# The square root's seed moved to ScalarE, and the channels' direct way turned into a diagonal product

## The chip, the cores and the metric

The kernel runs on one core of a Trainium2 chip. The metric is the device time of one launch in microseconds (us). A core has five engines that run their own queues of instructions in order: PE (matrix products; PEld is its loading of weights), DVE (vector), ACT (scalar, with activation functions), POOL (general purpose) and SP, which here only issues transfers (DMA).

## The reference, cut to what matters

The first layer is a state-space block, done twice (`NLAYERS = 2`) on 4 batches of 4096 positions with 96 channels. Inside, there are 192 channels and 16 states for each:

```
mu = seq.mean(-1, keepdims=True)
var = ((seq - mu) ** 2).mean(-1, keepdims=True)
h = (seq - mu) * jax.lax.rsqrt(var + EPS) * ln_g + ln_b
xz = h @ in_w
xs, z = jnp.split(xz, 2, axis=-1)
...
xc = jax.nn.silu(xc)                      # after a causal convolution of 4 taps
delta = jax.nn.softplus(dt @ dt_w + dt_b)
dA = jnp.exp(delta[..., None] * A)
dBx = delta[..., None] * Bm[:, :, None, :] * xc[..., None]
hstates = jax.lax.associative_scan(comb, (dA, dBx), axis=1)[1]
y = jnp.einsum('blds,bls->bld', hstates, Cm) + Dp * xc
y = y * jax.nn.silu(z)
return y @ out_w
```

The change is in two places of this: `rsqrt(var + EPS)`, and the term `Dp * xc`, the channels' direct way past the states. A quadratic layer and two pairs of Fourier and feed-forward layers follow. The change does not touch them.

## The kernel before, in words

The function `_mamba` holds the state-space stage. The work is cut into 32 units `(ch, l, pr)`: a chunk of 512 positions (`TC`), a layer, and a pair of batches. The channels of a pair fill three groups `k` of 128 partitions: `k = 0` and `1` hold the first 128 channels of either batch, `k = 2` the last 64 of both.

A unit is scanned in 24 steps: three groups `k`, four rounds `r`, two halves `h`. A step does this:

- SP loads a copy of `delta` spread over the states into a tile `a` (`copies`, line 434), and ACT turns it into the decay `exp(delta * A)` (`decays`, line 452).
- PE spreads `delta * xc` over the states into a PSUM tile `pq` of two banks, of which there are three (`broadcasts`, line 447). DVE multiplies it by `B` (`product`, line 457). In the steps with `k < 2`, `h = 0` and odd `r` ("apart"), a loaded copy `db` is multiplied on POOL instead, and ACT writes the decay into the `pq` tile.
- DVE runs two scans over 512 positions into `hs` (`scans`, line 470). POOL multiplies the states by `C` into `hc` (line 476). Both `hs` and `hc` have two tiles of two steps each.
- ACT keeps the last state for the next chunk (`states`, `hst`, line 480), and PE sums the states into the channels with a matrix `red`, four products into four quarters of one PSUM tile `py` (`reduce`, line 488). There is one `py` tile; it is summed over eight steps.
- After the eighth, `gate` reads it. DVE makes `y = Dp * xcv + py` (line 496), and POOL multiplies by `silu(z)` (line 497). The gates of the three groups come at the steps 10, 18 and 2 of the next unit.

Beside the steps run other chains, cut into pieces by `yield`; `Side.slot` lets one piece through in each step. `norm` makes the normalised input of a coming unit: PE subtracts the mean and sums the squares (`mm_v`, line 212), ACT adds epsilon (`ve`, line 221), DVE makes the seed of the inverse square root by shifting the bits of the float (lines 223 to 225, `it`, `r`, `vh`), and POOL refines it three times (lines 227 to 230); PE spreads the result (`mm_r`, line 240), and DVE multiplies (`hn`, line 249). `front` multiplies by the input weights (`mm_i`, lines 264 and 267), ACT empties each bank into `xcv` and `zs` (lines 275 and 277), and then come SiLU (lines 279 and 280), the products `mm_dbl` (lines 287 and 290), `delta` (line 315 and softplus, line 601), and `du`, `ux`, `uy` and `ul` (lines 339 to 355), which feed the spreading of `delta * xc`. `tail` multiplies by the output weights (`mm_o`, lines 369 to 371; the results are `s` or `ft`). `xcv` has two tiles. All products of `norm`, `front` and `tail` share one PSUM bank, `mm`.

The order on every engine is the order in which the program is written (`manual_schedule`). SP's queue issues nearly all transfers, so a transfer that waits for its data holds back those behind it; the copies of `ul` into `ux` and `uy` (line 345) are such.

Of the kernel before, what the change touches and what calls it, by code (L numbers as in the profile page):

```python
# [9 lines left out]
F32 = mybir.dt.float32  # L10
F32R = mybir.dt.float32r
I32 = mybir.dt.int32
# [3 lines left out]
AF = mybir.ActivationFunctionType  # L16
ALU = mybir.AluOpType
# [6 lines left out]
NL = 2  # L24
# [3 lines left out]
TC = 512  # L28
# [14 lines left out]
def _load(nc, pool, src, shape, name, dtype=F32):  # L43
    t = pool.tile(shape, dtype, name=name, tag=name)
    nc.sync.dma_start(t, src)
    return t


def _mamba(ctx, tc, io, w, fd, fstats, xsums):
# [9 lines left out]
    nc = tc.nc  # L59
    wp = ctx.enter_context(tc.tile_pool(name="mw", bufs=1))  # L60
# [5 lines left out]
    ps_y = ctx.enter_context(tc.tile_pool(name="mpsy", bufs=1, space=PSUM))  # L66
    vec, ident = w["vec"], w["ident"]
# [23 lines left out]
    red = _load(nc, wp, io["k_red"].rearrange("c (j m) -> c j m", j=4), [128, 4, 32], "red")  # L91
    ctr = _load(nc, wp, io["k_center"], [C, C], "ctr")
    low = _load(nc, wp, io["k_low"], [128, 2], "low")
    mean1 = wp.tile([C, 1], F32, name="mean1", tag="mean1")
    nc.gpsimd.memset(mean1, 1.0 / C)

# [56 lines left out]
    def col(l, n, k):  # L153

        at = l * 6 + n * 2 + (k == 2)
        return pv[:, at : at + 1]


    units = []
    for ch in range(NCH + 1):  # L160
# [6 lines left out]
    seq, made, ys = {}, {}, {}  # L167
    pqs, das, dbs, hss, hcs, pys = {}, {}, {}, {}, {}, {}

    def tag(unit):  # L170
        return "_".join(map(str, unit))

    def mm(nm, unit, shape=None):
        return ps_mm.tile(shape or [128, TC], F32, name=f"mm_{nm}{tag(unit)}", tag="mm")

    def tl(nm, unit, shape, dtype=F32, bufs=1, to=None):
        return work.tile(shape, dtype, name=f"{nm}_{tag(unit)}", tag=to or nm, bufs=bufs)
# [9 lines left out]
    def norm(unit):  # L187

        ch, l, pr = unit
        bs = (2 * pr, 2 * pr + 1)  # L190
        xc, sqs, ps = {}, {}, {}

        def centred(n):
            xc[n] = tl(f"xc{n}", unit, [C, TC])
            nc.scalar.copy(xc[n], ps[n])
            sqs[n] = tl(f"sq{n}", unit, [C, TC])
            nc.scalar.activation(sqs[n], xc[n], AF.Square)

        for n, b in enumerate(bs):
            ps[n] = mm(f"xc{n}", unit, [C, TC])  # L200
            nc.tensor.matmul(ps[n], ctr, seq[b, ch, l], start=True, stop=True)
            if l == 0:
                nc.scalar.activation(
                    tl("xs", unit, [C, TC], to=f"sq{n}"), seq[b, ch, 0], AF.Identity, accum_out=xsums[:, b, ch : ch + 1]
                )
            yield
            centred(n)
            yield "free" if n == 0 else "gap"
        p_v = mm("v", unit, [128, 8])
        for n in range(2):  # L210
            for j in range(4):
                nc.tensor.matmul(
                    p_v[:, n * 4 + j : n * 4 + j + 1], sqs[n][:, j * 128 : (j + 1) * 128], mean1, start=True, stop=True
                )
        yield
        ve = tl("ve", unit, [128, 8])
        it = tl("it", unit, [128, 8], I32)
        r = tl("r", unit, [128, 8])
        vh = tl("vh", unit, [128, 8])
        a = tl("ra", unit, [128, 8])  # L220
        nc.scalar.activation(ve, p_v, AF.Identity, bias=w["eps"])
        yield "gap"
        nc.vector.tensor_single_scalar(it, ve.bitcast(I32), 1, op=ALU.logical_shift_right)
        nc.vector.tensor_scalar(r.bitcast(I32), it, -1.0, float(0x5F3759DF), ALU.mult, ALU.add)
        nc.vector.tensor_scalar(vh, ve, -0.5, None, ALU.mult)
        for _ in range(3):
            nc.gpsimd.tensor_tensor(a, r, r, ALU.mult)
            nc.gpsimd.tensor_tensor(a, a, vh, ALU.mult)
            nc.gpsimd.tensor_scalar(a, a, 1.5, None, ALU.add)
            nc.gpsimd.tensor_tensor(r, r, a, ALU.mult)  # L230
        if ch:
            for b in bs:
                hn = hn_buf[b, l]
                nc.scalar.copy(hn[:, 0:3], hn[:, TC:])
        yield "gap"
        yield "gap"
        for n, b in enumerate(bs):
            p = mm(f"r{n}", unit, [C, TC])
            for j in range(4):
                nc.tensor.matmul(  # L240
                    p[:, j * 128 : (j + 1) * 128],
                    r[:, n * 4 + j : n * 4 + j + 1].to_broadcast([128, C]),
                    ident,
                    start=True,
                    stop=True,
                )
            yield
            yield
            nc.vector.tensor_tensor(hn_buf[b, l][:C, 3:], p, xc[n], ALU.mult)
            yield "free"  # L250
# [159 lines left out]
    def name(s):  # L410
        unit, k, r, h = steps[s]
        return f"{tag(unit)}_{k}_{r}_{h}"
# [69 lines left out]
    def reduce(g):  # L482
        unit, k, r, h = steps[2 * g]
        if r == 0:
            pys[unit, k] = ps_y.tile([128, TC], F32, name=f"py_{name(2 * g)}", tag="py")
        hc = hcs.pop(g)
        for i in range(4):
            nc.tensor.matmul(  # L488
                pys[unit, k][32 * (i // 2 + i % 2 * 2) :][:32], red[:, r, :], hc[:, i, :], start=(r == 0), stop=(r == 3)
            )  # L490

    def gate(g):
        unit, k, r, h = steps[2 * g]
        xcv, zs = made[unit][0:2]
        y = work.tile([128, TC], F32, name=f"y{k}_{name(2 * g)}", tag=f"y{k}")
        nc.vector.scalar_tensor_tensor(y, xcv[:, k, :], col(unit[1], 2, k), pys.pop((unit, k)), ALU.mult, ALU.add)
        (nc.gpsimd if 2 * g + 2 < n_steps else nc.vector).tensor_tensor(y, y, zs[:, k, :], ALU.mult)
        ys[unit, k] = y

# [34 lines left out]
    with tc.manual_schedule():  # L534
        for n in (0, 1):
            load(units[n])
        side.front = [weights(0), norm(units[0]), front(units[0])]
        side.drain()
        for s in range(5):
# [7 lines left out]
        for s in range(n_steps + NS):  # L547
# [5 lines left out]
            if at == 0:  # L553
                if n + 1 < len(units) and n + 1 not in late:
                    side.front += ([norm(units[n + 1])] if n == 0 else []) + [front(units[n + 1])]
                    side.norm += [weights(1)] * (n == 0)
            if at == 22 and n + 1 == len(units):
                side.tail.append(way_out(units[n]))
            if at == 3 and 0 < n < len(units):
                if n + 1 in late:  # L560
                    side.front = [tail(units[n - 1]), norm(units[n + 1]), front(units[n + 1])]
                else:
                    side.tail.append(tail(units[n - 1]))
# [5 lines left out]
            if s + 2 < n_steps:  # L569
                unit, k, r, h = steps[s + 2]  # L570
# [9 lines left out]
            if s % 2 == 1 and 2 < s <= n_steps + 1:  # L580
                reduce(s // 2 - 1)
# [5 lines left out]
            if live and s + 5 < n_steps:  # L587
                unit, k, r, h = steps[s + 5]
# [5 lines left out]
            if s % 8 == 2 and 2 < s <= n_steps + 2:  # L594
                gate(s // 2 - 2)
# [800 lines left out]
@with_exitstack  # L1396
def kernel(ctx: ExitStack, tc: tile.TileContext, io, out):
    nc = tc.nc
    cp = ctx.enter_context(tc.tile_pool(name="common", bufs=1))
    dp = ctx.enter_context(tc.tile_pool(name="scratch", bufs=1, space=DRAM))  # L1400
    w = _shared(nc, cp, io)
    p2 = [[dp.tile([2 * C, TC], F32, name=f"p2_{b}_{n}", tag=f"p2_{b}_{n}") for n in range(NCH)] for b in range(B)]
    fd = [dp.tile([C, L], F32, name=f"fd_{b}", tag=f"fd_{b}") for b in range(B)]
    with tc.tile_pool(name="stats", bufs=1) as fp:
        fstats = fp.tile([C, B, NCH, 6], F32, name="fstats", tag="fstats")
        xsums = fp.tile([C, B, NCH], F32, name="xsums", tag="xsums")
        with ExitStack() as c:
            _mamba(c, tc, io, w, fd, fstats, xsums)
        with ExitStack() as c:
            _back(c, tc, io, w, fd, fstats, xsums, p2, out)  # L1410
# [143 lines left out]
```

## Time and profile before

| what | value |
|---|---|
| time, median of 3 runs | 5290.37 us (5288.55 to 5313.22) |
| the profiled execution's own time | 5277.23 us |
| its span in the profile | 5275.4 us |
| mean TensorE clock granted over the span | 0.802 |
| PE busy | 4055.2 us, 77% |
| DVE busy | 4432.0 us, 84% |
| ACT busy | 2695.1 us, 51% |
| POOL busy | 2988.1 us, 57% |

The page gives the busy time of each engine, the span in slices, the transfers, the chain of work that ended last, and the costliest groups of instructions. A group's line has the line of the code, the engine, the operation, output and inputs, their shapes, and the count; then the busy time in us, the mean of one in ns, and the idle time of the engine just before, with what ended it. The state-space stage takes some 3125 us of the span; the table's shares are over all stages.

### The profile page before, as it was taken

The page shows a single profiled execution, that of the slowest core. Times are in us where ns is not written, and L with a number is a line of the kernel's source. Part 1 is how long each engine was busy: PE and PEld are TensorE (multiplying, and loading weights), DVE is VectorE, ACT ScalarE, POOL GpSimd, SP SyncE. Part 2 cuts the span into 40 slices and gives each one's busy share as a digit, 9 for nine tenths or more (in the row PEclk, how much of TensorE's full clock was granted, in tenths as well). Part 3 has the DMA queues.
Part 4 walks back from the last instruction along what each step waited for, and adds up shares of the span by engine and source line. Part 5 has one row for each costly group of instructions (what it writes and reads, how often), then busy time and mean ns, then how long its engine had stood idle before and what let it go on. Part 6 is the DMA issues. An engine that isn't in the chain of part 4 may idle for free.

```text
span 5275.4 us, 52716 instructions
## 1 busy us (share of the span) xinstructions
PE 4055.2 (77%) x15440; PEld 1763.8 (33%) x15440; DVE 4432.0 (84%) x5735; ACT 2695.1 (51%) x5085; POOL 2988.1 (57%) x2104
## 2 busy tenths in 40 slices
PE   4676767777777777777777636899898889989776
PEld 2122222222222222222222102345454555545565
DVE  2879999999999999999999777878787978787655
ACT  3465656656565565656656420023453545444566
POOL 2778888888888888888888761002130312112122
PEclk7677767677786777767777658999999999999976
DMA  4778878788888878788788674553324233322110
GB/s 99 171 171 197 198 187 203 194 196 201 197 192 195 200 190 194 189 195 202 184 201 202 148 192 139 171 170 100 99 85 145 90 102 94 98 90 76 57 33 21
DMA packets 314045, 800.18 MB, mean 152 GB/s; under 512 B 52247, under 2 KB 58106, under 8 KB 312702
## 3 DMA queue, kind: packets, MB, share of 16 engines
q1 hardware_dynamic: 310174, 790.53, 59.2%
q10 hardware_dynamic: 3584, 6.29, 0.4%
q8 instruction: 123, 2.02, 0.2%
q14 instruction: 164, 1.34, 0.1%
HBM read 703.83 MB, written 67.63 MB: 146 GB/s over the span
## 4 chain that ended last, share of the span: by engine, by line
PE 26%; DVE 26%; issue 17%; ACT 11%; POOL 8%; DMA 5%; SPq 1%; DVEq 0%; POOLq 0%; ACTq 0%
DVE hs L470 12%; PE py L895 10%; DVE pq L457 6%; ACT a L452 3%; DMA a<-ddl 3%; POOL hc L476 3%; PE mm_i L264 2%; DVE z L880 2%; DVE a L1110 2%; PE px L1177 2%; PE ph L1092 2%; PE pa L1078 2%; PE py L488 1%; POOL t L1248 1%; POOL o L1246 1%
## 5 line engine op out<-in xcount | busy, mean ns | idle before, releaser
L476 POOL TENSOR_TENSOR hc<-hs,bc 128x1024 f32<-128x1024 f32 x767 | 1804.8, 2360 | 365.8 <-DVE hs L470 350.0
L470 DVE TENSOR_TENSOR_SCAN hs<-a,hst,pq 128x512 f32<-128x512 f32 x1280 | 1571.9, 1261 | 28.9 <-ACT hst L480 12.8
L895 PE MATMUL py<-z,wk 128*96 128x512 f32 x2304 | 1113.5, 613 | 25.8 <-issue 14.3
L452 ACT ACTIVATE a<-a,aneg 128x512 f32<-128x512 f32 x1280 | 849.4, 712 | 309.5 <-DMA a<-ddl 307.4
L880 DVE TENSOR_TENSOR z<-cp,cp 128x512 f32<-128x512 f32 x1152 | 792.5, 714 | 183.9 <-PE py L895 169.3
L457 DVE TENSOR_TENSOR pq<-pq,bc 128x1024 f32<-128x1024 f32 x640 | 772.9, 1208 | 156.9 <-PE pq L447 156.9
L488 PE MATMUL py<-hc,red 128*32 128x512 f32 x3072 | 609.0, 865 | 14.3 <-POOL hc L476 14.3
L895 PEld LDWEIGHTS py<-z,wk 128*96 128x96 f32 x2304 | 366.5, 169 | 447.7 <-issue 315.6
L447 PE MATMUL pq<-uy,sel 64*128 64x512 f32 x768 | 253.4, 654 | 257.1 <-DVE hs L470 204.7
L1145 POOL MEMSET zz<- 96x2 f32 x16 | 1.6, 98 | 740.8 <-ACT zz L1154 739.4
L264 PE MATMUL mm_i<-hn,wk 97*128 97x512 f32 x512 | 348.7, 817 | 92.5 <-ACT xcv L275 59.7
L1246 POOL TENSOR_TENSOR o<-o,fb 128x384 f16<-128x384 f16 x64 | 70.1, 1096 | 549.4 <-ACT o L1251 549.4
L470 DVE TENSOR_TENSOR_SCAN hs<-pq,hst,db 128x512 f32<-128x512 f32 x256 | 324.8, 1269 | 58.1 <-issue 36.1
L452 ACT ACTIVATE pq<-a,aneg 128x512 f32<-128x512 f32 x256 | 177.1, 692 | 366.6 <-DVE hs L470 336.4
L457 POOL TENSOR_TENSOR db<-db,bc 128x1024 f32<-128x1024 f32 x128 | 301.8, 2358 | 21.8 <-DMA db<-ddu 20.3
L447 PE MATMUL pq<-ux,sel 64*128 64x512 f32 x512 | 166.4, 637 | 186.1 <-DVE hs L470 171.8
L447 PEld LDWEIGHTS pq<-uy,sel 64*128 64x128 f32 x768 | 93.8, 238 | 550.8 <-DVE hs L470 372.1
L264 PEld LDWEIGHTS mm_i<-hn,wk 97*128 97x128 f32 x512 | 117.2, 254 | 297.3 <-issue 204.2
L1177 PE MATMUL px<-bd,a 128*96 128x128 f32 x1024 | 148.6, 294 | 67.5 <-DVE a L1110 57.1
L1146 POOL TENSOR_TENSOR zz<-zz 96x256 f32<-96x256 f32 x128 | 122.3, 955 | 135.5 <-ACT zz L1153 83.4
L447 PEld LDWEIGHTS pq<-ux,sel 64*128 64x128 f32 x512 | 61.4, 232 | 384.7 <-DVE hs L470 275.4
L275 ACT ACTIVATE xcv<-mm_i,pvec 128x512 f32<-128x512 f32 x96 | 65.8, 685 | 213.8 <-PE mm_i L264 108.8
(286 smaller groups left out, 6645.8 us busy)
## 6 DMA issues: line engine op xcount, KB each, us to landing
a<-ddl SPq DMA_DIRECT2D x768, 512.0 KB, 7.3
cp<-p SPq DMA_DIRECT2D x480, 192.0 KB, 2.7
db<-ddu SPq DMA_DIRECT2D x128, 512.0 KB, 7.6
bc<-ddb SPq DMA_DIRECT2D x64, 512.0 KB, 8.4
cp<-p SPq DMA_DIRECT2D x480, 64.0 KB, 2.6
ddl<-dl SPq DMA_DIRECT2D x128, 192.0 KB, 3.5
tw_k_fwd<-in_k_fwd SPq DMA_DIRECT2D x64, 256.0 KB, 3.6
tw_k_inv<-in_k_inv SPq DMA_DIRECT2D x64, 256.0 KB, 3.0
```

Of the source, the lines that this page charges most:

```text
L264: nc.tensor.matmul(p, wt[:, 0:128], hn_buf[bs[k], l][:, cols], **f)
L447: nc.tensor.matmul(pqs[s][:, i, :], sel[rows, r, :], made[unit][6][k][h][rows], start=True, stop=True)
L452: nc.scalar.activation(to[:, i, :], das[s][:, i, :], AF.Exp, scale=acol(s, i))
L457: engine.tensor_tensor(t, t, bc(unit, 2, k, h), ALU.mult)
L470: nc.vector.tensor_tensor_scan(hss[g][:, at, :], d0[:, i, :], d1[:, i, :], hst[pr, l, g % 12][:, at : at + 1], ALU.mult, ALU.add)
L476: (nc.gpsimd if s + 1 < n_steps else nc.vector).tensor_tensor(hcs[g][:, sl, :], hss[g][:, sl, :], bc(unit, 3, k, h), ALU.mult)
L488: nc.tensor.matmul(pys[unit, k][32 * (i // 2 + i % 2 * 2) :][:32], red[:, r, :], hc[:, i, :], start=(r == 0), stop=(r == 3))
L880: nc.vector.tensor_tensor(zs[n], cps[q, r0], cps[q, r1], ALU.mult)
L895: nc.tensor.matmul(pys[q], wk[k // KG][:, k % KG, :], zs.pop(n), start=(k == 0), stop=(k == NE - 1))
L1146: nc.gpsimd.tensor_tensor(z0[:, :, 0, :], z0[:, :, 0, :], z1[:, :, 0, :], ALU.add)
L1177: nc.tensor.matmul(p[:, j, :], a2[i % 2][:, kk, :], tabs["bd"][:, int(kk > 0), :], start=True, stop=True)
L1246: nc.gpsimd.tensor_tensor(o2.rearrange("p j c -> p (j c)"), os.pop(g), d["fb2"], ALU.add)
```

## The change

Three things are different.

The seed of the inverse square root is made by ACT. It was an integer shift, a subtraction from a constant and a scaling on DVE; it is now one activation that reads the float's bits as an integer, multiplies by -0.5 and adds the constant, which is a column `magic`. `vh` (minus half of the variance) is made by ACT too, in the same piece as `ve`.

The direct term becomes a product on PE. A table `skip` is built once on POOL: for each layer, and for `k < 2` and `k = 2`, the 128 values of `Dp` stand on the diagonals of four 32 by 32 blocks. `reduce` opens the sum of each `py` tile with four products of such a block with 32 rows of `xcv`; the products with `red` then add to it.

`gate` has only to copy `py` out, and ACT does that; POOL's multiplication follows as before.

```diff
+    magic = wp.tile([128, 1], F32, name="magic", tag="magic")
+    nc.gpsimd.memset(magic, float(0x5F3759DF))
...
+    skip = wp.tile([128, 2 * NL, 32], F32, name="skip", tag="skip")
+    for l in range(NL):
+        for k in (0, 2):
+            for q in range(4):
+                rows = slice(32 * q, 32 * q + 32)
+                nc.gpsimd.tensor_scalar(skip[rows, 2 * l + k // 2, :], ident[rows, rows], col(l, 2, k)[rows], None, ALU.mult)
...
         ve = tl("ve", unit, [128, 8])
-        it = tl("it", unit, [128, 8], I32)
...
         nc.scalar.activation(ve, p_v, AF.Identity, bias=w["eps"])
+        nc.scalar.activation(vh, ve, AF.Copy, scale=-0.5)
         yield "gap"
-        nc.vector.tensor_single_scalar(it, ve.bitcast(I32), 1, op=ALU.logical_shift_right)
-        nc.vector.tensor_scalar(r.bitcast(I32), it, -1.0, float(0x5F3759DF), ALU.mult, ALU.add)
-        nc.vector.tensor_scalar(vh, ve, -0.5, None, ALU.mult)
+        nc.scalar.activation(r.bitcast(I32), ve.bitcast(I32), AF.Identity, bias=magic, scale=-0.5)
...
         if r == 0:
-            pys[unit, k] = ps_y.tile([128, TC], F32, name=f"py_{name(2 * g)}", tag="py")
+            p = pys[unit, k] = ps_y.tile([128, TC], F32, name=f"py_{name(2 * g)}", tag="py")
+            for q in range(4):
+                rows = slice(32 * q, 32 * q + 32)
+                nc.tensor.matmul(p[rows], skip[rows, 2 * unit[1] + (k == 2), :], made[unit][0][rows, k, :], start=True, stop=False)
...
-                pys[unit, k][32 * (i // 2 + i % 2 * 2) :][:32], red[:, r, :], hc[:, i, :], start=(r == 0), stop=(r == 3)
+                pys[unit, k][32 * (i // 2 + i % 2 * 2) :][:32], red[:, r, :], hc[:, i, :], start=False, stop=(r == 3)
...
-        nc.vector.scalar_tensor_tensor(y, xcv[:, k, :], col(unit[1], 2, k), pys.pop((unit, k)), ALU.mult, ALU.add)
+        nc.scalar.copy(y, pys.pop((unit, k)))
```

Apart from these, the instructions of every engine stand in the order in which they stood before, and SP's queue is the same instruction for instruction. The bursts of four products come at the steps 3, 11 and 19 of a unit, right ahead of the first products with `red`; ACT's copies come at the steps 10, 18 and 2, right behind a copy of the last state.

## The prediction

> **What bounds the kernel now.** I read in this order: stretches of 500 us, groups by line, the list of waits, then the order of time in one unit. A unit is the work on one chunk of two batches in one layer; it takes 24 steps, and a step is two decayed copies, one product and two scans.
>
> First the stretches. Columns: bounds, length, busy us (instructions) of PE, PEld, DVE, ACT, POOL, then clock, DMA share, GB/s.
> ```profile
> 500.00:1000.00 500.00, 377.16 (x1287) 123.58 (x1291) 474.73 (x419) 297.35 (x506) 435.21 (x267) 0.73 0.83 198
> 1500.00:2000.00 500.00, 371.32 (x1266) 124.21 (x1259) 472.78 (x419) 300.11 (x513) 435.57 (x280) 0.71 0.83 197
> ```
> The reader sees DVE busy 95% and POOL 87%, while ACT has 40% to spare. The whole change lies in this stage, which ends near 3125 us; the rest of the 5275 us is untouched. On these two lines alone, taking work off DVE should pay in full.
>
> Then the groups that the change removes (busy us, mean ns, idle before).
> ```profile
> L496 DVE SCALAR_TENSOR_TENSOR y<-xcv,pvec,py 128x512 f32<-128x512 f32 x96 | 69.5, 723 | 4.2 <-PE mm_o L369 2.5 <-PE py L488 1.6
> L224 DVE TENSOR_SCALAR r<-it 128x8 int32<-128x8 int32 x32 | 62.3, 1946 | 1.1
> L225 DVE TENSOR_SCALAR vh<-ve 128x8 f32<-128x8 f32 x32 | 33.8, 1056 | 0.0
> L223 DVE TENSOR_SCALAR it<-ve 128x8 int32<-128x8 int32 x32 | 24.8, 775 | 32.2 <-ACT ve L221 32.2
> ```
> Three instructions on 8 columns cost 120.9 us, though the first unit's, with POOL idle, took 0.17 us each. In later units they stand behind POOL's long products.
>
> Last, one unit in order of time, with its step 18 ending at 2433.4. Start, us, operation, and in brackets the idle time before it. POOL, without the small refinement instructions between 2439.7 and 2443.0:
> ```profile
> 2434.91 2.35 POOL L476 TENSOR_TENSOR hc<-hs,bc 128x1024 f32<-128x1024 f32 x1
> 2437.22 1.26 POOL L497 TENSOR_TENSOR y<-y,zs 128x512 f32<-128x512 f32 x1
> 2438.43 1.27 POOL L339 TENSOR_TENSOR du<-dl,xcv 128x512 f32<-128x512 f32 x1
> ...
> 2443.02 2.35 POOL L476 TENSOR_TENSOR hc<-hs,bc 128x1024 f32<-128x1024 f32 x1
> ...
> 2450.09 4.86 POOL L476 TENSOR_TENSOR hc<-hs,bc 128x1024 f32<-128x1024 f32 x2
> 2454.90 1.27 POOL L355 TENSOR_TENSOR ul<-du,ux 128x512 fp32r<-128x512 f32 x1
> ```
> POOL has no gap from 2430.1 to 2456.2, just where DVE makes the seed. The third `ul` ends at 2456.2; behind it stand four `ux`/`uy` copies on SP's queue, then the load of `a` for step 5 of the next unit (2459.7). ACT must decay that before it empties the front's first bank (line 275). PE follows:
> ```profile
> 2467.85 3.78 PE L264 MATMUL mm_i<-hn,wk 97*128 97x512 f32 x4 [1.49 <-ACT xcv L275]
> 2471.56 0.80 PE L447 MATMUL pq<-uy,sel 64*128 64x512 f32 x2
> 2472.29 1.93 PE L488 MATMUL py<-hc,red 128*32 128x512 f32 x8
> ...
> 2502.85 0.79 PE L447 MATMUL pq<-uy,sel 64*128 64x512 f32 x2
> 2503.57 1.93 PE L488 MATMUL py<-hc,red 128*32 128x512 f32 x8
> 2505.44 1.08 PE L287 MATMUL mm_dbl<-xcv,xp 128*64 128x512 f32 x4
> 2506.45 1.08 PE L290 MATMUL mm_dbl<-xcv,xp 64*64 64x512 f32 x4
> ```
> DVE waits for `pq` at 2472.4, 2479.6 and 2503.7 (0.72, 1.01, 3.62 us) and at 2510.35 (1.90 us) for a scan buffer that ACT's `hst` copy releases; on ACT that copy stands behind the emptying of `mm_dbl`. So from the front's first bank (about step 2) to step 14 the unit runs through PE and ACT, from step 14 to 17 through DVE, and from 17 to the next step 5 through POOL, SP and a transfer. **DVE's 95% is several near-equal paths, not one bound.**
>
> **What the Trainium skill says.** *SBUF — State Buffer*, "Who interferes with whom": a VectorE `tensor_scalar` in a two-port mode and a GpSimd instruction exclude each other, and the later one waits for the whole of the other. The trace agrees: 0.17 us alone, a median of 2.28 us for `r` beside a 2.36 us product. *TensorE: Matmul & The Clock Gate*, Part 1: activity releases a half-rate clock. Agrees: eight `py` instructions take 1.06 or 1.93 us. *TensorEngine Tiling (Array Packing)*, "Key Properties": separate tiles run in parallel. Agrees for two diagonal 64 by 64 tiles into one bank (line 290: four instructions in 1.08 us); four 32 by 32 tiles, and the drain the page names on a change of mode, are not in this trace.
>
> **Part by part.** Sums are against the profiled execution (5277.2 us, of which 5275.4 are span), 13 us under the median of 5290.4; I add 13 at the end.
>
> *Off DVE:* 3 seed instructions and 3 gates a unit, 190.4 us in 32 units, some 179 us after overlaps of about 0.06 us each. Three of a unit's gates stand at steps 2, 10 and 18, the seed at 19: none between 14 and 17, where DVE alone sets the time.
>
> *On ACT:* per unit `vh` 0.19 (like `hst`, 188 ns), `r` 0.26 (like `ve`, 264 ns, an activation with a bias column), three copies at 0.58 (line 277): 2.2 us, 70 us in all. ACT is idle 40%, and the copies stand behind `hst`, before waits of 2 to 5 us. I cost them at nothing. `r` is done at about 2437, before POOL's refinement at 2439.7; should it be late, POOL's unbroken stretch grows by that much. Behind a waiting copy stand the decays, prepared two steps ahead (7 us).
>
> *On POOL and SP:* 16 multiplications of 32 by 32 at the start, about 0.23 us each (line 229), in an idle stretch of 16.96 us: nothing. SP's queue and all transfers stay as they are.
>
> *On PE:* 3 bursts of 4 products a unit, each first in the sum of `py`, right behind a `pq` and ahead of whatever PE does next. By line 488, 1.06 us at full clock and 1.93 at half, if the four run beside one another.
>
> *Step 19's burst* falls where PE idles (5.8 us before 2442): nothing.
>
> *Steps 19 to 5.* Without the seed DVE runs ahead until its two scan buffers stop it, and the unbroken POOL stretch still ends the same time after step 17. What is won is at the front's first bank, which in 21 units also waited for the gate of step 2 to finish reading `xcv` (32.8 us). In 14 of the 30 units after the first step 18 to step 2 lasts 33.6 to 34.8 us instead of 33; there I take 1.7 us won, in the other 16 0.4 us: mean 1.01.
>
> *Step 3's burst* sits behind that bank. In 15 of 30 units the way from step 2 to 10 takes 27.7 us or more instead of 26.2, PE being late: there I charge 1.5 us (between 1.06 and 1.93), in the rest 0.4: mean 0.95.
>
> *Step 11's burst* stands between the `pq` of step 13 and `mm_dbl`, ahead of ACT's `hst`, ahead of the scan of step 14: all of it. In 13 units PE is then at half clock: (13 x 1.93 + 17 x 1.06)/30 = 1.44.
>
> *Once:* DVE's waits for `ve` go (32.2 us, five times); the wait of `hn` for `mm_r` comes next and I let it take 20: 12 won.
>
> Sum: 30 x (0.95 + 1.44 - 1.01) - 12 = 29.4 us more: 5307, on the median's footing **5320 us**. Bounds: bursts hidden, 30 x -1.01 - 12 = -42; bursts at half clock throughout, 30 x (1.93 + 1.93 - 0.4) = +104. The drain on a change of mode I take as 0; it gains nothing.
>
> **The rivals.**
>
> *Faster: DVE is the bound after all.* For it: 95% busy, and a longest pause for POOL of a few us. Against it: POOL's unbroken stretch. Price: 179 us less a sixth, about 5140. A milder form: with the seed's stall gone PE no longer idles 5.8 and 2.7 us there and enters the front at full clock, saving 1.8 us on the 3.78 us at 2467.85. It decides once that saving exceeds the 1.38 us net a unit; with another 1.8 us from a warm `mm_o` (2.02 against 1.10 us, twice) a unit gains 2.2: 5211 if in every unit, 5247 if in two of three.
>
> *No change.* The bursts go into PE's idle quarter, most of which is waiting for scans (365 us): 5250 to 5300.
>
> *The tiles do not run together.* A burst is then four times as long, 3 us more twice a unit: 180 us more, about 5500.
>
> *The change doesn't do what it says:* the seed still on DVE, or a table load for the new activations; Identity and Copy already stand between Exp and Silu with no load of their own (63 loads at line 452). Unlikely.
>
> **How the numbers follow.** Slower as forecast 0.44 (own range 5300 to 5370), tiles one by one 0.05, no change 0.28, faster by the warm clock 0.13, DVE the bound 0.10. A measurement of this kernel can tell about 0.5%, 26 us. Faster (under 5264): 0.23. Slower (over 5317): 0.47, a little of the forecast's own range lying below. Same: 0.30. The range leaves out the two extreme cases and a little more: 5220 to 5385.
>
> **What would show it.** Right: DVE below 92% with its idle time before `pq` and `hs` grown; POOL still unbroken from step 17 to the third `ul`; each burst 1.0 to 1.9 us; step 14 later after `mm_dbl`. Wrong: DVE still at 95% over a shorter stage (DVE was the bound), a mean clock clearly above 0.73 in the stage (the warm clock pays), or bursts of 4 us.

## The result, and the profile after

| what | before | after |
|---|---|---|
| time, median | 5287.37 us | 5340.08 us (5311.62 to 5370.94) |
| the profiled execution's own time | 5277.23 us | 5370.94 us |
| mean TensorE clock over the span | 0.802 | 0.825 |

The changed kernel takes 1.0095 times as long, with a 95% interval of 1.0067 to 1.0122: about 50 us slower. The profiled execution after is the slowest of its eight and lies 31 us above their median, about 1 us in each of 30 units; the one before lies 10 us below. The two traces together therefore overstate the difference.

First the stretches of 500 us again, after. Columns: bounds, length, busy us (instructions) of PE, PEld, DVE, ACT, POOL, then clock, DMA share, GB/s.
```profile
500.00:1000.00 500.00, 386.63 (x1371) 117.00 (x1369) 434.05 (x379) 301.49 (x529) 428.14 (x276) 0.79 0.80 191
1500.00:2000.00 500.00, 388.39 (x1377) 116.05 (x1373) 431.11 (x375) 307.20 (x530) 420.00 (x260) 0.79 0.80 192
```
DVE fell from 95% to 87% and 86%, and the granted clock rose from 0.73 and 0.71 to 0.79 in both. Yet each stretch holds less work of the steps: the transfers went down from 198 and 197 to 191 and 192 GB/s.

Then the groups that are new (busy us, mean ns, idle before).
```profile
L496 PE MATMUL py<-xcv,skip 32*32 32x512 f32 x768 | 173.2, 991 | 19.2 <-ACT y L507 19.2
L508 POOL TENSOR_TENSOR y<-y,zs 128x512 f32<-128x512 f32 x95 | 120.6, 1269 | 66.5 <-ACT y L507 66.2
L507 ACT COPY y<-py 128x512 f32<-128x512 f32 x96 | 55.5, 579 | 2.3 <-PE py L499 2.3
L232 ACT ACTIVATE r<-ve,magic 128x8 int32<-128x8 int32 x32 | 9.5, 298 | 0.0
L230 ACT ACTIVATE vh<-ve 128x8 f32<-128x8 f32 x32 | 6.7, 209 | 1.0
```
All of them last about as long as they were costed. What the sum did not have are two waits for ACT's copy, at the right ends of the first two lines: PE's burst waits 19.2 us for the copy to free `py`, and POOL's product waits 66.2 us for it, with the next `hc` queued behind on POOL.

The waits of POOL, ACT and DVE in the state-space stage, after (total us, times, longest):
```profile
POOL hc L483 <- PE py L499: 103.2, 48, 4.1
...
ACT pq L459 <- DMA a<-ddl: 265.2, 30, 10.0
...
ACT pq L459 <- DVE hs L477: 49.0, 49, 6.8
...
DVE pq L464 <- PE pq L454: 222.6, 109, 5.0
```
Before, the first of these is not in the list at all, and the others read:
```profile
ACT pq L452 <- DVE hs L470: 336.4, 90, 7.4
ACT pq L452 <- DMA a<-ddl: 18.6, 2, 11.4
...
DVE pq L457 <- PE pq L447: 108.2, 76, 4.4
```
Read ACT's two lines together: before, ACT's decays into `pq` waited for DVE's scans; now they wait for the load of `a`. DVE was relieved and another releaser comes last: 355.0 us in all became 314.2 us.

PE in one unit after, around step 11, in order of time:
```profile
2481.54 0.79 PE L454 MATMUL pq<-uy,sel 64*128 64x512 f32 x2
2482.26 1.93 PE L496 MATMUL py<-xcv,skip 32*32 32x512 f32 x8
2484.12 1.94 PE L499 MATMUL py<-hc,red 128*32 128x512 f32 x8
2485.99 1.20 PE L294 MATMUL mm_dbl<-xcv,xp 128*64 128x512 f32 x4
2487.12 1.08 PE L297 MATMUL mm_dbl<-xcv,xp 64*64 64x512 f32 x4
```
The burst lies exactly where the prediction put it, between the `pq` and `mm_dbl`, and lasts the 1.93 us that eight such products take at the lower clock. POOL in the same unit, at that time:
```profile
2476.45 1.26 POOL L508 TENSOR_TENSOR y<-y,zs 128x512 f32<-128x512 f32 x1 [1.09 <-ACT y L507]
2477.66 2.34 POOL L483 TENSOR_TENSOR hc<-hs,bc 128x1024 f32<-128x1024 f32 x1
2479.96 2.35 POOL L464 TENSOR_TENSOR db<-db,bc 128x1024 f32<-128x1024 f32 x1
2486.22 2.35 POOL L483 TENSOR_TENSOR hc<-hs,bc 128x1024 f32<-128x1024 f32 x1 [3.91 <-PE py L499]
```
The last line is the chain in small: `py` ends late behind the burst, so a tile of `hc` comes free late, and POOL stands for 3.91 us.

To compare kernels I cut each unit at three events that every trace shows: the emptying of the front's first bank by ACT (line 282 after), the first product of `mm_dbl` on PE (line 294), and `ve` on ACT. The table gives the mean stretches over 26 units, in us. They come from one execution each, so a few tenths of a us mean nothing.

| kernel | first bank to `mm_dbl` | `mm_dbl` to `ve` | `ve` to the next first bank | unit |
|---|---|---|---|---|
| before | 36.20 | 21.74 | 35.09 | 93.0 |
| after | 40.19 | 21.62 | 34.16 | 96.0 |
| seed alone | 37.82 | 21.81 | 34.09 | 93.7 |
| direct way alone | 39.05 | 21.64 | 34.03 | 94.7 |
| no burst | 38.21 | 21.91 | 34.00 | 94.1 |
| neither burst nor ACT's copy | 38.09 | 21.92 | 34.10 | 94.1 |
| later `ul`, seed on DVE | 35.48 | 21.73 | 34.79 | 92.0 |
| later `ul`, seed on ACT | 37.96 | 21.88 | 31.83 | 91.7 |
| later `ul`, whole change | 38.99 | 21.69 | 31.35 | 92.0 |

The middle stretch, which holds the steps 14 to 17, is the same in all of them. The last one becomes 0.9 us shorter and the first 4.0 us longer, some 3 us when the slow profiled execution is allowed for.

### The profile page after: what moved, and what is told of

It reads as the page before. It is cut to its first block, busy times and chain, and to the rows that moved or that the text cites. A ratio compares the mean times of both kernels' runs of the same rounds, so it can differ in the third digit from the quotient of the medians.

```text
span 5368.9 us, 54230 instructions
## 1 busy us (share of the span) xinstructions
PE 4211.1 (78%) x16208; PEld 1761.8 (33%) x16208; DVE 4267.3 (79%) x5543; ACT 2747.0 (51%) x5245; POOL 2994.2 (56%) x2121
## 4 chain that ended last, share of the span: by engine, by line
PE 29%; DVE 15%; issue 15%; POOL 12%; ACT 11%; DMA 9%; SPq 2%; POOLq 0%; DVEq 0%; ACTq 0%
PE py L906 9%; DMA a<-ddl 7%; DVE hs L477 6%; POOL hc L483 5%; ACT a L459 4%; PE mm_i L271 3%; DVE pq L464 3%; PE py L499 2%; DVE z L891 2%; POOL du L346 2%; PE py L496 2%; DVE a L1121 2%; PE px L1188 2%; PE pa L1089 1%; PE ph L1103 1%
## 5 line engine op out<-in xcount | busy, mean ns | idle before, releaser
L906 PE MATMUL py<-z,wk 128*96 128x512 f32 x2304 | 1115.7, 613 | 26.8 <-issue 14.4
L499 PE MATMUL py<-hc,red 128*32 128x512 f32 x3072 | 647.0, 809 | 80.0 <-POOL hc L483 79.9
L271 PE MATMUL mm_i<-hn,wk 97*128 97x512 f32 x512 | 322.2, 762 | 151.0 <-ACT xcv L282 125.9
L499 PEld LDWEIGHTS py<-hc,red 128*32 128x32 f32 x3072 | 77.5, 121 | 391.4 <-issue 188.8
```

The lines of the kernel that those rows point to most:

```text
L271: nc.tensor.matmul(p, wt[:, 0:128], hn_buf[bs[k], l][:, cols], **f)
L499: nc.tensor.matmul(pys[unit, k][32 * (i // 2 + i % 2 * 2) :][:32], red[:, r, :], hc[:, i, :], start=False, stop=(r == 3))
L906: nc.tensor.matmul(pys[q], wk[k // KG][:, k % KG, :], zs.pop(n), start=(k == 0), stop=(k == NE - 1))
```

## The experiments

Every ratio is to the kernel before, run on the same chip; 0.1% is 5.3 us. Four kernels (neither burst nor ACT's copy, the copy first, and the later `ul` with the seed on DVE or on ACT) ran on one chip and all the others on a second one, so a comparison between these two sets goes through the ratios.

### The two halves of the change

The seed alone, put on the kernel before:
```diff
...
+        nc.scalar.activation(vh, ve, AF.Copy, scale=-0.5)
         yield "gap"
-        nc.vector.tensor_single_scalar(it, ve.bitcast(I32), 1, op=ALU.logical_shift_right)
-        nc.vector.tensor_scalar(r.bitcast(I32), it, -1.0, float(0x5F3759DF), ALU.mult, ALU.add)
-        nc.vector.tensor_scalar(vh, ve, -0.5, None, ALU.mult)
+        nc.scalar.activation(r.bitcast(I32), ve.bitcast(I32), AF.Identity, bias=magic, scale=-0.5)
```


> The kernel before, with the seed alone made on ScalarE (gates stay on DVE). Theory of the record: POOL's unbroken stretch from step 17 to the third ul hides what DVE gives up, so about 12 us are won once and nothing per unit: 0.998 of before (0.994 to 1.000), and the stretch from ve to the third ul stays at 23 to 24 us. Rival, DVE is the bound: its 121 us of seed instructions less a sixth come back, about -100 us, 0.981.

Measured: 1.001 (0.9994 to 1.0026). DVE went down from 95% to 88% and 90% in the two stretches, and nothing was won. That DVE is the bound by itself is refuted. Nor does the single gain of 12 us show in the total: the interval leaves room for 3 us. From `ve` to the next first bank the unit is 1.0 us shorter (35.09 to 34.09), and from there to `mm_dbl` it is 1.6 us longer.

The direct way alone: the changed kernel with the three DVE instructions of the seed in place again, the edit above the other way round.

> The changed kernel with the seed put back on DVE: the diagonal product and ScalarE's copy alone. Theory of the record: the bursts of steps 3 and 11 cost 0.95 and 1.44 us a unit and 1.01 come back, 41 us, and as the whole change measured +50 and the seed is worth -12, up to +62: 1.008 to 1.012 of before. Rival, DVE is the bound: the 69 us of gates leave it, -58 us, 0.989.

Measured: 1.0095 (1.0074 to 1.0117), the same as the whole change. What the change costs is the direct way.

### The burst and the copy

No burst: the four products are left out, and `red` opens the sum; the result then lacks the term `Dp * xc`.
```diff
-                nc.tensor.matmul(p[rows], skip[rows, 2 * unit[1] + (k == 2), :], ...)
...
-                ..., red[:, r, :], hc[:, i, :], start=False, stop=(r == 3)
+                ..., red[:, r, :], hc[:, i, :], start=(r == 0), stop=(r == 3)
```


> The changed kernel without the four diagonal products that open the sum (the term Dp*xc is left out); the seed and the copy stay on ScalarE. Theory of the record, the bursts on PE are what costs: all of the +50 goes and the won part shows, -42 us, 0.992 of before. Rival, ScalarE's copy as a new wait for POOL's y (66 us of waits in the trace after, with hc queued behind it) is what costs: most of the +50 stays, 1.005 to 1.010.

Measured: 1.0049 (1.0029 to 1.0069), between the two theories. By the middle values about half of the loss, 0.46% or 24 us, belongs to the bursts; the 42 us of gain that should then have shown did not.

The copy on DVE, bursts kept:
```diff
-        nc.scalar.copy(y, pys.pop((unit, k)))
+        nc.vector.tensor_copy(y, pys.pop((unit, k)))
```


> The changed kernel with py copied out by DVE instead of ScalarE; bursts and ScalarE's seed stay. Theory of the record, bursts: within 10 us of the changed kernel, 1.008 to 1.011 of before. Rival, the wait for ScalarE's copy costs: half or more of the +50 goes, 1.000 to 1.005. Third way: DVE is so near its limit that its 0.6 us three times a unit come on top: over 1.012.

Measured: 1.0073 (1.0051 to 1.0096). The copy's place on ACT costs some 0.2%, 12 us by the middle values, though the intervals of the two kernels overlap.

Both edits together:

> The changed kernel with the diagonal products taken out (the term Dp*xc is left out) and py copied out by DVE; only the seed on ScalarE and the shorter gate are left. If burst and copy are the two costs, and they add up (the bursts measured 0.46%, the copy 0.22%): 1.001 to 1.003 of before, like the seed alone at 1.001. If something else of the direct way costs, such as the bank of py held longer or the tile xcv let go of earlier: over 1.004.

Measured: 1.0032 (1.0018 to 1.0045). By their middle values the effects add up: taken in either order, the bursts are worth 0.41 and 0.46%, the copy 0.17 and 0.22%. The bursts' share is beyond doubt (this interval and that of the copy on DVE lie apart); the copy's is as large as the intervals are wide, and rests on both pairs pointing the same way. Some 0.2% stays above the seed alone; the intervals of the two overlap, so whether anything is there is open.

Is the copy late because it stands behind decays on ACT? Here it is written first in its step:
```diff
+            if s % 8 == 2 and 2 < s <= n_steps + 2:
+                out(s // 2 - 2)          # y and nc.scalar.copy, taken out of gate
             if s + 2 < n_steps:
                 unit, k, r, h = steps[s + 2]
```


> The changed kernel with ScalarE's copy of py written at the start of its step, ahead of the decays of the next steps, and POOL's product where it was. If the copy costs because it stands behind decays that wait for a transfer: POOL's waits for it (66 us) fall below 25 us, and 10 to 25 us are won on the changed kernel, 1.005 to 1.0075 of before. If it costs as such, or the decays now wait for py: no change or worse, 1.009 to 1.014.

Measured: 1.0133 (1.0102 to 1.0164), not better. In the trace POOL's `y` is gone from the long waits, but its `hc` waits longer for `py` (103.2 us in the changed kernel), and the second line is new (that kernel's waits of POOL and ACT):
```profile
POOL hc L483 <- PE py L499: 126.2, 41, 5.7
...
ACT y L506 <- PE py L499: 29.2, 9, 7.6
```
`py` itself is late. Moved forward, the copy waits for it in front of the decays, which stand behind it in ACT's order.

### Which burst costs

The prediction gave each of a unit's three bursts a price by its place. These three kernels have one of them three times over (its term then counts three times in the result):
```diff
+            for n in range(3 if k == 0 else 1):      # k == 1, k == 2 in the other two
                 for q in range(4):
...
-                ..., start=True, stop=False)
+                ..., start=n == 0, stop=False)
```


> The changed kernel with the burst of step 3 three times over (its term Dp*xc counts three times); the others as they are. Record: 0.95 us a unit for one burst there, between 0.4 and 1.5, so two more at 1.06 to 1.93 each all on the way, 60 to 115 us: 1.021 to 1.031 of before. Rival, by the run without bursts: some 23 us for all three bursts of a unit, 8 us each, two more cost 16 us: 1.011 to 1.014.

> The same with the burst of step 11. Record: all of it lies between pq and mm_dbl on the unit's way, 2 x 1.44 us in 30 units, 86 us: 1.023 to 1.028. Rival, 8 us a burst wherever it stands: 1.011 to 1.014. If step 11 is the costly place and step 3 is not, this run is over 1.018 and the one of step 3 under 1.015.

> The same with the burst of step 19. Record: PE idles there, so two more cost nothing: 1.008 to 1.011, as the changed kernel. Rival, 8 us a burst wherever it stands: 1.011 to 1.014; if more PE time at step 19 delays the front that follows: over 1.014.

| burst trebled at | ratio | two more bursts, over the changed kernel | one burst, per unit |
|---|---|---|---|
| step 3 | 1.0163 (1.0134 to 1.0193) | +36 us | 0.60 us |
| step 11 | 1.0189 (1.0157 to 1.0221) | +50 us | 0.83 us |
| step 19 | 1.0072 (1.005 to 1.0094) | -12 us | nothing |

(36 us is 0.68% of 5287 us; divided by two bursts and 30 units, 0.60 us.) The places were right, the sizes were not: nothing at step 19, and at step 3 and step 11 about six tenths of the forecast. That step 11 is dearer than step 3 is not shown, since the two intervals overlap.

### What hides the seed

The prediction says that POOL's unbroken stretch from step 17, then SP's queue, then the load of `a` for step 5 set the unit's pace where the seed was. The next edit shortens that way and touches nothing of the change. The second and third `ul` and the copies behind them, which the kernel emits at steps 21 to 23, are emitted by the unit that uses them, at steps 1 and 7 (their transfers at steps 2 and 8); the first unit is left alone.
```diff
+            if live and n:
+                dus, cut, parts = put_off[units[n]]
+                if at in (1, 7):
+                    rests(units[n], 1 + at // 7, dus, cut)    # ul on POOL
+                elif at in (2, 8):
+                    cross(cut[at // 8 + 1], parts)            # its four transfers on SP
             if live:
                 scans(s)
```
With the seed on DVE, as before:

> The kernel before (seed and gates on DVE), with the second and third ul, and the transfers behind each, put off from steps 22 and 23 to steps 1 and 7 of the unit that needs them. Theory of the record, a unit's way goes from step 17 through POOL's unbroken stretch and SP's queue to the load of a for step 5: 2 x 1.27 us of POOL and two sets of four transfers leave it, up to 2.5 us in each of 30 units, 0.986 to 0.994; the wait of SP for ul (183 us) shrinks by half or more. Rival, DVE at 95% is the bound: no change, 0.999 to 1.001, or slower where the two ul come in the way of a product of POOL.

Measured: 0.9977 (0.9961 to 0.9993), a gain of 12 us and not of 30 to 75. SP's wait for `ul` did not shrink but grew to 538 us: the transfers now stand earlier in the queue than their data are ready. That sign was badly chosen: in the faster kernel that follows the same wait is 663 us.

With the seed on ACT:

> The same, with the seed on ScalarE. Theory of the record: with POOL's stretch shorter, DVE is the next to set the end there, and the seed that DVE no longer makes (some 4 us of DVE a unit, part of it waiting for POOL) now pays: 5 to 40 us under the same kernel with the seed on DVE, 0.980 to 0.992 of before. Rival: the seed is worth nothing wherever POOL stands, and both are alike within 0.2%.

Measured: 0.9927 (0.99 to 0.9954), **39 us faster than the kernel before**. Now the seed pays: 0.50%, 26 us, where without the later `ul` it was worth nothing. The stretch from `ve` to the next first bank is 31.83 us against 34.09 us for the seed alone, 2.26 us less; two `ul` take 2 x 1.27 = 2.54 us. With the seed on DVE the same edit shortened it by 0.30 us only. So two ways of nearly the same length ran side by side there, POOL with SP's queue and DVE with the seed: cutting one alone is worth 1.0 or 0.3 us in this stretch, cutting both 3.3 us. (The seed's 1.0 us is lost again further on; see the account of the prediction.)

POOL in one unit of that kernel, where three `ul` stood in a row of products before:
```profile
2424.07 1.27 POOL L356 TENSOR_TENSOR ul<-du,ux 128x512 fp32r<-128x512 f32 x1
2425.30 9.39 POOL L483 TENSOR_TENSOR hc<-hs,bc 128x1024 f32<-128x1024 f32 x4
2435.12 2.36 POOL L464 TENSOR_TENSOR db<-db,bc 128x1024 f32<-128x1024 f32 x1 [0.44 <-DMA db<-ddu]
2437.44 2.36 POOL L483 TENSOR_TENSOR hc<-hs,bc 128x1024 f32<-128x1024 f32 x1
2439.75 1.28 POOL L356 TENSOR_TENSOR ul<-du,ux 128x512 fp32r<-128x512 f32 x1
```
The second `ul` now comes 14.4 us after the first one's end; POOL is as busy as ever, but the load of `a` no longer stands behind the `ul`.

The whole change with the later `ul`:

> The whole change together with the later ul. Theory: the direct way's cost lies on the way from the front's first bank to mm_dbl and stays, 45 us over the seed alone with the later ul (0.9927): 1.000 to 1.003 of before. Rival: once POOL's stretch is broken up, DVE is what sets the end, and its gates taken off pay as the seed did: under 0.993.

Measured: 0.9945 (0.992 to 0.997). The middle value lies between the two expectations, and the interval reaches into the rival's. The direct way, which costs 0.85% on top of the seed in the old order (1.001 to 1.0095), costs 0.18% here, which these intervals can't tell from nothing. Its bursts are still in the stretch to `mm_dbl` (38.99 us against 37.96 us), but the rest of the unit gives half of that back (31.35 against 31.83 us). And behind the first bank PE gives back two thirds of what the bursts take: they fill 3.1 us of its time there, and its other products take 30.0 us instead of 32.1 us. Why it gives back more in this order was not taken apart further.

## Why the prediction was right, and where its sum was not

The time came 20 us over the forecast of 5320 us, on the forecast side and inside its own range. The signs named beforehand came too: DVE at 87%, its wait for `pq` doubled (108.2 to 222.6 us), bursts of at most 1.93 us, a later `mm_dbl`, and POOL without a gap where the seed is refined. In one unit after:
```profile
2509.30 2.36 POOL L483 TENSOR_TENSOR hc<-hs,bc 128x1024 f32<-128x1024 f32 x1
2511.62 1.27 POOL L508 TENSOR_TENSOR y<-y,zs 128x512 f32<-128x512 f32 x1
...
2524.52 4.67 POOL L483 TENSOR_TENSOR hc<-hs,bc 128x1024 f32<-128x1024 f32 x2
2529.14 1.28 POOL L362 TENSOR_TENSOR ul<-du,ux 128x512 fp32r<-128x512 f32 x1
```
From 2509.30 to the end of the third `ul` at 2530.4 POOL does not pause.

The sum is less good than its result, for two errors of opposite sign met in it: a gain that didn't last, and bursts charged three times too high. That the total came within 20 us is in good part luck. Term by term:

- **DVE's 179 us are hidden.** Right in the total, and for the seed's part shown from both sides: 0.1% slower for the seed alone, 0.5% faster once POOL's way is cut. (The gates' part was not tested by itself.) POOL's stretch behaved nearly as forecast: from `ve` to the end of the third `ul` the 26 units mostly take 23.3 or 24.5 us before, 23.7 on average, and with the seed alone 23.1 us, never more than 23.3.
- **The front's first bank, -1.01 us a unit.** This is the step that failed. The bank did come 1.0 us earlier after `ve`, with the seed alone as well. But the prediction left the way behind the bank as it was, the bursts apart, and booked the 1.01 us as won. That way grew by itself: by 1.6 us with the seed alone, where PE has no burst. Without burst and without ACT's copy, where the gain should have stood alone, the kernel was at 1.0032 and not at 0.992. The next table has the stretch from the first bank to `mm_dbl`, in us, means over the same 26 units:

| kernel | PE busy | PE idle | granted clock |
|---|---|---|---|
| before | 30.0 | 6.2 | 0.85 |
| later `ul`, seed on DVE | 29.5 | 6.0 | 0.87 |
| seed alone | 31.8 | 6.0 | 0.81 |
| no burst | 32.1 | 6.1 | 0.80 |
| neither burst nor ACT's copy | 31.9 | 6.2 | 0.81 |
| later `ul`, seed on ACT | 32.1 | 5.9 | 0.80 |
| after | 34.1, of which bursts 3.2 | 6.1 | 0.81 |

In all but the last, PE starts 98 products in this stretch in every one of the 26 units, and it stands idle for the same 6 us. What grew with the seed on ACT is the time of these same products, by some 2 us, while the clock over the stretch fell from 0.85 or 0.87 to about 0.80. The two go together: 30.0 us times 0.853/0.807, the clocks before and with the seed alone, is 31.7 us, and 31.8 us were measured. That is where the gain went. Just in front of the first of them PE now waits 4.3 us for ACT to empty the bank, where it waited about 2 us. PE's waits before, and then with the seed alone:
```profile
PE mm_i L264 <- ACT xcv L275: 70.1, 59, 3.6
...
PE mm_i L264 <- ACT xcv L275: 136.4, 60, 6.3
```
Whether this wait is what lowers the clock was not tested. Some 30 us too much was counted as won, and the 12 us won once were not seen either.

- **The bursts, +0.95 and +1.44 us.** The places were right. Two more at each place cost 0.60 and 0.83 us apiece, and taking all three away gives back 22 to 24 us in 30 units, 0.7 to 0.8 us a unit against the 2.39 us charged. The burst of step 19 goes into PE's idle time: from `ve` to the first bank PE idles 12.3 us without bursts and 11.5 us with them, in a stretch of the same length within 0.2 us. The other two do not: up to `mm_dbl` PE idles 6.1 us in both kernels. There the two bursts take 3.2 us, and the 98 other products take 30.9 us instead of 32.1 us, so more than a third is returned by products that run faster. (The rest, 2.0 us, still holds the 1 us a unit by which the profile after is slow.) I charged nearly the full length and left out what PE gives back.
- **ACT's copies, 0.** Too low: 0.17 to 0.22%, 9 to 12 us, if the middle values hold. I looked at what follows the copy on ACT, and not at who waits for it: POOL, with `hc` behind, and PE's burst.
- **The clock.** A clock clearly above 0.73 was to show the forecast wrong, because a warm PE would pay. It rose to 0.79, and the kernel was slower. The seed alone already brings 0.76 and 0.77 at an unchanged time. The mean over the stage misled: with the seed alone the clock rose from 0.61 to 0.74 between `ve` and the first bank, where PE is idle 13 or 14 us of 34 or 35, and fell from 0.85 to 0.81 behind the bank, where PE is busy five sixths of the time. So the rival's warm PE at the front did not come about; the front ran at a lower clock.
- **The tiles.** *TensorEngine Tiling (Array Packing)*, "Key Properties", in the Trainium skill says that separate tiles run in parallel. The trace agrees for four 32 by 32 tiles that write four quarters of one bank: eight instructions with a mean of 991 ns each are done in 1.93 us. The drain on a change of mode that the prediction took as 0 doesn't show as a pause: the burst starts 0.72 us after a `pq` of 0.79 us (2481.54 and 2482.26 above), just as a `py` did before (2471.56 and 2472.29 in the prediction's lines).

So the right sum would read: seed 0.1%, bursts 0.4 to 0.5%, the copy 0.2%, and 0.2% that stays open; together the 0.95% measured.

## What to carry to other kernels

Where several engines come to the same pace, taking work off the busiest is worth what the second way leaves: the seed was worth nothing until two small operations of POOL were put off, and then 26 us. When one stretch of a period gets shorter, measure the next one too: here PE took longer for the same products behind it and gave the gain back, and a mean clock that rose over the stage hid that it fell where PE sets the pace. And of an operation that moves to an idle engine ask who waits for its result and what is queued behind that one; the engine's idle share doesn't say it.

## What the runs showed of the hardware that was not expected

An activation on ScalarE that reads the float's bits as integers and writes integers takes 298 ns for 128 by 8 values, against 209 ns for the plain scaling beside it. Multiplying a 32 by 32 block on POOL by a column of scalars takes 402 ns, where 230 ns had been estimated from a block of 128 by 8:
```profile
L165 POOL TENSOR_SCALAR skip<-ident,pvec 32x32 f32<-32x32 f32 x16 | 6.4, 402 | 1.2
```
And the clock that PE is granted in the stage rose from about 0.72 to 0.77 when three DVE instructions of 8 columns went to ScalarE, with no change in PE's own work. It rose and fell by stretch: 0.61 to 0.74 between `ve` and the first bank, 0.85 to 0.81 from there to `mm_dbl`. Why was not tested.
